# Loading every fifth x tile in three pieces of 100, 20 and 8 rows on fewer DMA engines

## The chip, the cores and the metric

The kernel runs on one core of one Trainium2 chip. A core has a matmul engine (PE), a vector engine (DVE), a scalar engine (ACT), a queue engine (SP) and sixteen DMA engines that carry every transfer between device memory (DRAM) and on-chip memory (SBUF). The metric is device time in microseconds, as a median of several runs. Every run below was fast, that is, within 1.5% of the fastest run of the same kernel. A profiled span is 1.2 to 2.4 us shorter than the timed median of the same kernel, so I compare spans with spans and times with times.

## The reference, cut to what matters

```python
i_idx, j_idx = np.triu_indices(32, k=1)          # 496 pairs of 32 fields
vi = inputs[:, i_idx, :]                         # inputs: (4096, 32, 64)
vj = inputs[:, j_idx, :]
vdotw = jnp.einsum('bpd,pde->bpe', vi, W)        # W: (496, 64, 64)
return (vdotw * vj).reshape(B, -1)               # (4096, 31744), float32
```

The output is 520 MB. The inputs are 33.6 MB (x) and 8.1 MB (W). Each pair needs one small matrix product and one elementwise product.

## The kernel before

The batch is cut into 32 tiles of 128 rows. For each tile, x is loaded to SBUF, transposed by PE, and multiplied with the weights. DVE multiplies the product in PSUM (PE's output memory) by x and writes it to a ring (a buffer that is filled in turn and used again) in SBUF, and five stores take the tile from the ring to DRAM. ACT issues the x loads; SP issues the weight loads and the stores. The ring holds a little under one tile's output (28160 of 31744 columns), so DVE has to wait until an old store has landed before it may write over its place. There are two x buffers.

```python
STORES = [[0, 1], [2, 3], [4, 5], [6, 7, 8], [9, 10, 11, 12, 13, 14, 15]]
PREFETCH_AT = [5, 6]
RING = 28160
...
    def load_x(t):
        xt = xpool.tile([P, F * D], F32, tag="x", name=f"x_{t}")
        nc.scalar.dma_start(out=xt, in_=x[ts(t, P), :])
        return xt
...
    xs = {0: load_x(0)}
    for p in range(NPR):
        ...                                             # 16 weight loads on SP
    for t in range(NT):
        xt, xT = xs.pop(t), xTs.pop(t)
        if t + 1 < NT:
            xs[t + 1] = load_x(t + 1)
        for s, group in enumerate(STORES):
            ...
            for p in group:
                if t + 1 < NT and p in PREFETCH_AT:
                    transpose_x(...)                    # the next tile's x, on PE
                ...                                     # matmuls, DVE products into the ring
            nc.sync.dma_start(out=out[ts(t, P), o0 : o0 + store_w[s]], in_=osb)
```

Of the kernel before, what the change touches and what calls it, by code (L numbers as in the profile page):

```python
# [1 line left out]

# [6 lines left out]

F32 = mybir.dt.float32  # L10
ALU = mybir.AluOpType

P = 128
BANK = 512

STORES = [[0, 1], [2, 3], [4, 5], [6, 7, 8], [9, 10, 11, 12, 13, 14, 15]]
PREFETCH_AT = [5, 6]
RING = 28160


@with_exitstack
def pair_bilinear_kernel(
    ctx: ExitStack,
    tc: tile.TileContext,
    x: bass.AP,
    w: bass.AP,
    out: bass.AP,
    F: int,
    D: int,
):  # L30
















    nc = tc.nc
    B = x.shape[0]
    NT = B // P
    NPR = F // 2  # L50

    width = [(F - 1 - i) * D for i in range(F)]
    off = [sum(width[:i]) for i in range(F)]
    woff = [sum(width[0 : 2 * p : 2]) for p in range(NPR)]
    store_w = [sum(width[2 * p] + width[2 * p + 1] for p in g) for g in STORES]

    const = ctx.enter_context(tc.tile_pool(name="const", bufs=1))
    xpool = ctx.enter_context(tc.tile_pool(name="x", bufs=2))
    xtpool = ctx.enter_context(tc.tile_pool(name="xT", bufs=2))
    psum = ctx.enter_context(tc.tile_pool(name="ps", bufs=4, space=bass.MemoryType.PSUM))  # L60

    ident = const.tile([P, P], F32, tag="ident", name="ident")
    make_identity(nc, ident)

    def runs(tl, a, b, n):

        ap = tl[:, a : a + n]
        return bass.AP(ap.tensor, ap.offset, [list(ap.ap[0]), [b - a, 2], list(ap.ap[1])])

    def load_x(t):  # L70
        xt = xpool.tile([P, F * D], F32, tag="x", name=f"x_{t}")
        nc.scalar.dma_start(out=xt, in_=x[ts(t, P), :])
        return xt

    def transpose_x(xT, t, xt, g):

        n = 2 * BANK // P
        pt = psum.tile([P, 2 * BANK], F32, tag="ps", name=f"pt_{t}_{g}")
        for c in range(n):
            nc.tensor.transpose(pt[:, ts(c, P)], xt[:, ts(n * g + c, P)], ident)  # L80
        nc.scalar.copy(xT[:, ts(g, 2 * BANK)], pt)  # L81

    def new_xT(t):
        return xtpool.tile([P, NPR * P], F32, tag="xT", name=f"xT_{t}")

    ring = const.tile([P, RING], F32, tag="ring", name="ring")
    at = 0
    xs = {0: load_x(0)}

    w_sb = []  # L90
    for p in range(NPR):
        wp = const.tile([P, width[2 * p]], F32, tag=f"w{p}", name=f"w{p}")
        nc.sync.dma_start(out=wp, in_=w[:, woff[p] : woff[p] + width[2 * p]])
        w_sb.append(wp)

    xTs = {0: new_xT(0)}
    for g in range(2):
        transpose_x(xTs[0], 0, xs[0], g)
# [6 lines that stand above are left out]
            if at + store_w[s] > RING:  # L105
                at = 0
            osb = ring[:, at : at + store_w[s]]
            at += store_w[s]
            o0 = off[2 * group[0]]
            for p in group:  # L110
                if t + 1 < NT and p in PREFETCH_AT:
                    if t + 1 not in xTs:
                        xTs[t + 1] = new_xT(t + 1)
                    transpose_x(xTs[t + 1], t + 1, xs[t + 1], PREFETCH_AT.index(p))
                for c0 in range(0, width[2 * p], BANK):
                    pm = psum.tile([P, 2, BANK], F32, tag="ps", name=f"pm_{t}_{p}_{c0}")
                    n = [max(0, min(BANK, width[2 * p + h] - c0)) for h in range(2)]
                    for h in range(2):
                        if n[h]:
                            nc.tensor.matmul(  # L120
                                pm[:, h, : n[h]],
                                xT[h * D : (h + 1) * D, ts(p, P)],
                                w_sb[p][h * D : (h + 1) * D, c0 : c0 + n[h]],
                                start=True,
                                stop=True,
                            )
                    o = [off[2 * p + h] - o0 + c0 for h in range(2)]
                    xj = [(2 * p + h + 1) * D + c0 for h in range(2)]
                    if n[0] == n[1]:
                        nc.vector.tensor_tensor(  # L130
                            runs(osb, o[0], o[1], n[0]),
                            pm[:, :, : n[0]],
                            runs(xt, xj[0], xj[1], n[0]),
                            ALU.mult,
                        )
                    else:
                        for h in range(2):
                            if n[h]:
                                nc.vector.tensor_tensor(  # L139
                                    osb[:, o[h] : o[h] + n[h]],  # L140
                                    pm[:, h, : n[h]],
                                    xt[:, xj[h] : xj[h] + n[h]],
                                    ALU.mult,
                                )
            nc.sync.dma_start(out=out[ts(t, P), o0 : o0 + store_w[s]], in_=osb)


# [33 lines left out]
```

## Time and profile before

| | before |
|---|---|
| time, median | 1341.3 us |
| span of the profiled run | 1339.7 us |
| DMA, mean share of sixteen engines | 98.8% |
| DVE, PE busy | 88%, 86% |
| last engine's end after the others' | 10.3 to 10.7 us |

The DMA share is a mean over sixteen engines and cannot tell whether one of them is behind. For that, each engine has to be read by itself; the prediction below tells how the packet records are laid end to end into sixteen chains. In each chain the stores come in program order, eight rows and a small semaphore packet (it reports the landing) for each store, and this settles most ambiguities. Where two chains are at the same point at the same nanosecond they may be swapped; the slow one can be told by its long rows. A chain has no number: numbers of engines in this document come from the skill's rule for which engines a load uses, which the prediction cites, and no trace shows them.

### The profile page before, as it was taken

Reading aid. Unit: us, or ns where it says so; the run is one execution under the profiler, and the core shown is the slowest. Engines: PE = TensorE matmul, PEld = TensorE weight load, DVE = VectorE, ACT = ScalarE, POOL = GpSimd, SP = SyncE. Lnnn points to the kernel's source line nnn. Section 1 sums busy time; section 2 is a strip of 40 time slices with the busy share of each in tenths; the row PEclk is TensorE's granted clock in tenths of the full one; section 3 lists DMA queues with packets and bytes.
Section 4 is the critical chain, followed back from the end, with each engine's and each line's share of the span. In section 5 each row is a group of like instructions: output and inputs, shape, how many; then the busy total and the mean of one; then the engine's idle time right before and its main releaser. Section 6 shows DMA issues by size and latency. Waiting matters only on the chain.

```text
span 1339.7 us, 13755 instructions
## 1 busy us (share of the span) xinstructions
PE 1151.0 (86%) x5376; PEld 548.7 (41%) x5376; DVE 1177.4 (88%) x1664; ACT 66.1 (5%) x65; POOL 0.7 (0%) x6
## 2 busy tenths in 40 slices
PE   7998889888898888988888978889798897888992
PEld 3444344443343443443433534444344443444441
DVE  6999889888899988989888989899898997898993
ACT  1000000000000000000000000000000000000000
POOL 0000000000000000000000000000000000000000
PEclk9999889999999999989999899899898998998996
DMA  9999999999999999999999999999999999999996
GB/s 392 426 431 434 429 431 429 427 427 434 426 434 430 422 422 430 422 424 429 415 426 424 426 426 404 415 420 431 428 420 408 431 427 431 416 424 420 422 429 264
DMA packets 30017, 562.93 MB, mean 420 GB/s; under 512 B 3456, under 2 KB 3840, under 8 KB 5376
## 3 DMA queue, kind: packets, MB, share of 16 engines
q1 hardware_dynamic: 25344, 528.49, 92.6%
q10 hardware_dynamic: 4608, 33.56, 6.0%
q8 instruction: 42, 0.69, 0.2%
q14 instruction: 23, 0.19, 0.0%
HBM read 41.94 MB, written 520.09 MB: 420 GB/s over the span
## 4 chain that ended last, share of the span: by engine, by line
DMA 54%; DVE 23%; PE 11%; issue 9%; DVEq 0%
DMA out_dram<-ring 54%; DVE ring L130 15%; PE pm L120 9%; DVE ring L139 9%; PE pt L80 2%; DMA x<-in_x_dram 1%; DVEq L130 0%; DVEq L177 0%
## 5 line engine op out<-in xcount | busy, mean ns | idle before, releaser
L120 PE MATMUL pm<-w,xT 64*128 64x512 f32 (+7 forms) x4864 | 1083.2, 559 | 158.3 <-DVE ring L130 140.1
L130 DVE TENSOR_TENSOR ring<-pm,x 128x1024 f32<-128x1024 f32 x768 | 904.0, 1217 | 138.4 <-DMA out_dram<-ring 93.0
L120 PEld LDWEIGHTS pm<-w,xT 64*128 64x128 f32 x4864 | 487.7, 194 | 720.1 <-DVE ring L130 451.3
L139 DVE TENSOR_TENSOR ring<-pm,x 128x448 f32<-128x448 f32 (+6 forms) x896 | 330.2, 415 | 3.6 <-PE pm L120 2.9
L81 ACT COPY xT<-pt 128x1024 f32<-128x1024 f32 x64 | 64.8, 1012 | 1194.6 <-PE pt L80 1194.6
L80 PE MATMUL pt<-ident,x 128*128 128x128 f32 x512 | 76.5, 297 | 8.5 <-DMA x<-in_x_dram 8.5
L80 PEld LDWEIGHTS pt<-ident,x 128*128 128x128 f32 x512 | 61.0, 152 | 48.9 <-issue 35.3
L81 ACT ACT_TABLE_LOAD x1 | 1.3, 1283 | 1.7 <-PEq L173 1.7
masks.py:199 POOL TENSOR_SCALAR_AFFINE_SELECT ident<-ident 128x128 f32<-128x128 f32 x1 | 0.3, 292 | 0.1
masks.py:197 POOL MEMSET ident<- 128x128 f32 x1 | 0.2, 204 | 0.3 <-POOLq L173 0.3
L173 POOL MEMSET const-bfloat16-1.0<- 128x1 bf16 x1 | 0.1, 101 | 0.0
L173 POOL MEMSET const-uint8-127<- 128x1 uint8 x1 | 0.1, 101 | 0.0
L173 POOL MEMSET const-float32-0.0<- 128x1 f32 x1 | 0.1, 98 | 0.2 <-issue 0.2
L173 POOL MEMSET const-float32-1.0<- 128x1 f32 x1 | 0.1, 98 | 0.0
## 6 DMA issues: line engine op xcount, KB each, us to landing
out_dram<-ring SPq DMA_DIRECT2D x32, 3776.0 KB, 22.8
out_dram<-ring SPq DMA_DIRECT2D x32, 3264.0 KB, 21.8
out_dram<-ring SPq DMA_DIRECT2D x32, 3168.0 KB, 22.4
out_dram<-ring SPq DMA_DIRECT2D x32, 2912.0 KB, 22.3
out_dram<-ring SPq DMA_DIRECT2D x32, 2752.0 KB, 22.1
x<-in_x_dram ACTq DMA_DIRECT2D x32, 1024.0 KB, 14.2
w<-in_w_dram SPq DMA_DIRECT2D x1, 992.0 KB, 7.4
w<-in_w_dram SPq DMA_DIRECT2D x1, 928.0 KB, 11.7
```

Of the source, the lines that this page charges most:

```text
L80: nc.tensor.transpose(pt[:, ts(c, P)], xt[:, ts(n * g + c, P)], ident)
L81: nc.scalar.copy(xT[:, ts(g, 2 * BANK)], pt)
L120: nc.tensor.matmul(pm[:, h, : n[h]], xT[h * D : (h + 1) * D, ts(p, P)], w_sb[p][h * D : (h + 1) * D, c0 : c0 + n[h]], start=True, stop=True,)
L130: nc.vector.tensor_tensor(runs(osb, o[0], o[1], n[0]), pm[:, :, : n[0]], runs(xt, xj[0], xj[1], n[0]), ALU.mult,)
L139: nc.vector.tensor_tensor(osb[:, o[h] : o[h] + n[h]], pm[:, h, : n[h]], xt[:, xj[h] : xj[h] + n[h]], ALU.mult,)
L173: nc = bacc.Bacc("TRN2", target_bir_lowering=False, num_devices=1)
```

## The change

The intent to be read from it is to take load from the highest six DMA engines, in seven of the 32 tiles (1, 6, 11, 16, 21, 26, 31), and to give it to the lowest ten. The bytes stay the same.

```diff
+FEW = 5
+FEW_ROWS = [100, 20, 8]
...
-        nc.scalar.dma_start(out=xt, in_=x[ts(t, P), :])
+        r0 = 0
+        for n in FEW_ROWS if t % FEW == 1 else [P]:
+            nc.scalar.dma_start(out=xt[r0 : r0 + n, :], in_=x[t * P + r0 : t * P + r0 + n, :])
+            r0 += n
```

## The prediction

> **What bounds the kernel now.** I read the page's slices, queue rows and chain first, to see which resource is full; then the waits of the vector engine and of the store queue, to see who waits for whom; then the stretches; and last the packet records themselves, engine by engine.
>
> ```profile
> span 1339.7 us, 13755 instructions
> DMA  9999999999999999999999999999999999999996
> q1 hardware_dynamic: 25344, 528.49, 92.6%
> q10 hardware_dynamic: 4608, 33.56, 6.0%
> HBM read 41.94 MB, written 520.09 MB: 420 GB/s over the span
> DMA 54%; DVE 23%; PE 11%; issue 9%; DVEq 0%
> DMA out_dram<-ring 54%; DVE ring L130 15%; PE pm L120 9%; DVE ring L139 9%; PE pt L80 2%; DMA x<-in_x_dram 1%; DVEq L130 0%; DVEq L177 0%
> x<-in_x_dram ACTq DMA_DIRECT2D x32, 1024.0 KB, 14.2
> ```
>
> The DMA engines are busy in every slice but the last. q1 (stores and w) takes 92.6% of the time of sixteen engines, q10 (x) 6.0%; with 0.2% of instruction fetch that is 98.8%, or 1323.6 us of 1339.7 on the mean engine. The chain names a store in 54% of the span. PE (86%) and DVE (88%) come after it.
>
> ```profile
> DVE ring L130 <- DMA out_dram<-ring: 93.0, 53, 3.3
> DVE ring L130 <- PE pm L120: 45.4, 52, 13.2
> ...
> SPq L145 <- DVE ring L139: 1228.7, 159, 10.5
> ```
>
> The vector engine waits for ring space (a store's landing) 53 times, 93.0 us in all. The store queue then waits for the vector engine. So a store that lands late holds back the next store: the last of its sixteen shares counts.
>
> ```profile
> core 0: us, PE busy (x) PEld busy (x) DVE busy (x) ACT busy (x) POOL busy (x), PEclk, DMA share, GB/s
> 9.00:50.00 41.00, 38.49 (x189) 19.58 (x189) 36.55 (x53) 4.05 (x4) 0.00 (x0) 1.00 1.02 423
> 50.00:500.00 450.00, 395.49 (x1852) 189.03 (x1850) 405.39 (x574) 22.27 (x22) 0.00 (x0) 0.95 1.00 429
> 500.00:1000.00 500.00, 438.90 (x2048) 208.53 (x2045) 448.21 (x632) 24.29 (x24) 0.00 (x0) 0.95 0.99 422
> 1000.00:1320.00 320.00, 277.63 (x1292) 130.97 (x1292) 287.22 (x409) 14.17 (x14) 0.00 (x0) 0.95 0.99 422
> 1320.00:1340.00 20.00, 0.00 (x0) 0.00 (x0) 0.00 (x0) 0.00 (x0) 0.00 (x0) 0.56 0.39 169
> ```
>
> In these rows by stretch the DMA share is 1.00 and 429 GB/s up to 500 us, 0.99 and 422 GB/s from there. In the last 20 us no compute engine works and the DMA share is 0.39, so most engines are done while something still drains.
>
> The packet records do not name their engine, but one engine's packets follow each other within 4 ns, so I laid all 30030 end to end into sixteen chains (a reconstruction; fast chains may be swapped among themselves, a slow one is told by its durations). **One chain is slow and fifteen are alike.** The slow one is busy 1344.2 us, never idle once data flows, and ends last. The other fifteen are busy 1318.7 to 1325.1 us (mean 1321.9), idle 10.6 us on the mean in 9 to 23 pauses, the first at about 495 us of the span, and all end 10.3 to 10.7 us before the slow one. A store row of 30208 B takes 1155 ns on the slow engine and 1119 to 1125 on the others (3% more), one of 22016 B 843 against 820; an x row of 8192 B 314 against 309. The slow engine loses some 0.75 us per batch tile, the ring hides a skew of about 10 us, and after tile 12 the others wait for it. The 22.3 us between 1344.2 and 1321.9 are about the 10.6 us of pauses and the 10.5 us of tail.
>
> **What the Trainium skill says.** (1) "DMA: Bandwidth & Descriptors", section "Why a DMA increments its semaphore by 16 and not by 1": a DMA issued by SP or ACT runs on the largest k up to 16 that divides the slowest dimension, and on the lowest-numbered k; its example is 100 partitions on 10 engines. So 100, 20 and 8 rows run on engines 0-9, 0-9 and 0-7. The trace before has only 128-row loads, on sixteen. (2) Same page, "Latency and other measured facts": engines 7 and 15 are usually slower, with a best guess that ties it to software descriptor rings. The trace agrees that an engine is slow, but only one, and there is no software queue in it; which number it has the trace doesn't say. (3) Same page, "Where 436 GB/s comes from": 435.2 GB/s over sixteen ports, so 27.2 each. The fast engines' 30208 B in 1119 ns are 27.0: each engine is at its own ceiling, so rows cannot be sped up, only moved. (4) "SBUF — State Buffer", section "Door 1: The DMA port swizzle": the partitions decide which of sixteen ports a transfer uses. In the pieces several engines may write to one port; no run yet shows what it costs.
>
> **The change part by part.** No byte and no compute instruction is added. Tiles 1, 6, 11, 16, 21, 26 and 31, seven of 32, have three x loads in place of one. The instruction order shows 14 more on ACT, and none else.
> - Removed: the six highest engines lose 8 rows in each of seven tiles: 56 x 0.309 = 17.3 us (56 x 0.314 = 17.6 us on the slow engine).
> - Added: engines 0-7 get 10 + 2 + 1 = 13 rows for 8, so 7 x 5 x 0.309 = 10.8 us; engines 8 and 9 get 12, so 7 x 4 x 0.309 = 8.7 us.
> - Issues: 14 x 0.37 us on ACT, which is busy 5%: nothing. The semaphores of the pieces were used last by transfers of the tile before last, 41 us earlier, against a landing time of 22 us: no wait. At the start the third piece of tile 1 goes out after the copies at 13 us and is wanted at 30 us.
> - Moved: x comes later. Eight rows between store rows take 8.5 to 9.2 us, about 1.08 each, after some 5 us; thirteen make 5 + 14 = 19 us.
>
> ```profile
> 620.63 0.36 ACTq L72 DMA_DIRECT2D x<-in_x_dram  x1
> 644.21 1.01 ACT L81 COPY xT<-pt 128x1024 f32<-128x1024 f32 x1 [38.85 <-PE pt L80]
> ...
> 705.07 0.37 ACTq L72 DMA_DIRECT2D x<-in_x_dram  x1
> 723.83 1.01 ACT L81 COPY xT<-pt 128x1024 f32<-128x1024 f32 x1 [33.22 <-PE pt L80]
> ```
>
> In this timeline the copy follows eight transposes (1.1 us), so x is wanted 22.5 us after its issue in one tile and 17.6 in another. PE may wait up to 2 us in some of the seven tiles. DVE has 1340 - 1177 = 163 us to spare, 5 per tile, and two stores are in flight, so this should not reach the DMA engines.
>
> The sum rests on a choice: I take the slow engine to be among the six highest (the page says 7 or 15, and the change would be odd otherwise). Then its work falls to 1344.2 - 17.6 = 1326.6 us, and it would end 17.6 us earlier. Engines 0-7 rise to 1321.9 + 10.8 = 1332.7 us on the mean and become the bound: 1344.2 - 1332.7 = 11.5 us earlier than the slow one ended. The same by the ends: 10.5 us of tail, plus 10.6 us of pauses that go since the skew stays under what the ring hides, less 10.8 us, is 10.3 us. The busiest fast chain (1325.1, with fetches on it) would leave 8 us. Two things pull further, which I set against each other: rows of 23296 B took 865 ns on the fast engines in the first nine tiles and some 895 later, when the pauses had begun, so up to 4 us may come back; and the moved rows may take longer, or x may come late. I take 8.5 us, near the busiest chain: 1341.3 - 8.5 = 1332.8, so **1333 us**.
>
> **The rivals.**
> - *The slow engine is one of the lowest ten*, 7 for instance. It is then given 35 x 0.314 = 11 us more: 1352 us. For it: the skill names 7 as well. Against: one slow chain only, and the period of five fits a gap of 22 us for a high engine (it closes 17.6 + 10.8 = 28). Chance 1 in 7.
> - *The moved rows collide*: ten engines write partitions that several share by port, and the 7 x 128 = 896 moved rows (896 x 0.309 / 10 = 28 us on each of ten) take, say, a fifth longer, 5.5 us; or late x starves the stores. Then most of the gain is gone: 1338 to 1343 us. For it: the rows have no such layout before. Against: an x row is less than a third of an engine's time while x loads.
> - *Perfect balance*: all engines end at the mean, 1323.3 us of busy time for 1344.2 on the slow one, 21 us less: 1320 us at the very best. Nothing can give more, as each row is at its engine's ceiling.
>
> **Range and chances.** Over 2% faster means under 1314.5 us, below the mean busy time: all but excluded. Over 2% slower means 1368 us: it needs a low slow engine and collisions on top, 2%. The middle is 1333; 1327 is the 10 to 11.5 us of the sum with the 4 us of late rows on top; 1343 is the gain lost to collisions. The rival at 1352 (1 in 7) lies outside, which is most of the fifth that I leave out.
>
> **What would show it.** Right: the six high engines have x rows in 25 of 32 tiles, the slow chain is one of them, with busy time near 1327; the pauses and the 10 us tail of draining shrink; the share stays 1.00 after 500 us; DVE's 93.0 us of waiting for stores falls a little. Wrong if the slow chain carries 13-row loads, if x rows in the pieces take clearly over 309 ns, or if PE waits for x by tens of us.

## More of the kernel before

Tile 0 and tile 1 of x load at the start, beside the weights. From tile 2 on an x load has only stores beside it.

The records name the chip of each experiment: e1 to e4 ran on chip 3, e5 to e7 on chip 10, e8 and e9 on chip 5; for the first pair none is named. Each round had the kernel before beside it, and it took 1341.2 to 1341.35 us on all of them.

## The result, and the profile after

The changed kernel takes **1357.45 us** (1357.31 to 1357.88, four runs) against 1341.32 us in the same rounds: 16.1 us slower. The ratio is 1.012, with a 95% interval of 1.0103 to 1.0138. Ratios here are the mean time of one kernel's fast runs over that of the other's of the same rounds, so not quite the ratio of the medians that I quote. The class "within 2%" was right; the time lies outside the predicted range, and the sign was wrong.

From the page of the changed kernel (the span, the queue rows, the chain by line, and the x loads by size):

```profile
span 1355.2 us, 13789 instructions
...
q1 hardware_dynamic: 25344, 528.49, 92.2%
q10 hardware_dynamic: 4692, 33.56, 6.1%
...
HBM read 41.94 MB, written 520.09 MB: 415 GB/s over the span
...
DMA out_dram<-ring 51%; DVE ring L137 13%; PE pm L127 9%; DVE ring L146 8%; DMA x<-in_x_dram 5%; PE pt L87 2%; ACTq L78 0%; DVEq L137 0%; DVEq L184 0%
...
x<-in_x_dram ACTq DMA_DIRECT2D x25, 1024.0 KB, 14.2
x<-in_x_dram ACTq DMA_DIRECT2D x7, 800.0 KB
x<-in_x_dram ACTq DMA_DIRECT2D x7, 160.0 KB
```

The shares of the queues are as high as before in a span that is 15.5 us longer. The engines are still full, and yet they move only 415 GB/s for 420. The bytes are equal; q10 has 84 more packets, all of them the small semaphore packets of the pieces.

The first 33.5 us of the kernel before, by the view of stretches (its first slice in the page):

```profile
0.00:33.50 33.50, 24.16 (x111) 12.19 (x111) 20.34 (x25) 4.32 (x4) 0.70 (x6) 1.00 0.98 392
```

The same stretch of the changed kernel:

```profile
0.00:33.50 33.50, 22.28 (x100) 13.10 (x102) 18.56 (x22) 3.60 (x4) 0.70 (x6) 0.95 0.96 318
```

The last two numbers are the DMA share and the GB/s. The engines are as busy, at 318 instead of 392 GB/s, and DVE gets 22 products done instead of 25. In the run e2 below, which has the change in tile 1 alone, the clock of PE (the third number from the end) is 1.00 as before and the stretch is as slow, so the 0.95 of the changed kernel is not the cause:

```profile
0.00:33.50 33.50, 22.65 (x104) 12.66 (x106) 19.29 (x24) 4.32 (x4) 0.70 (x6) 1.00 0.95 318
```

The waits of the SP queue for the landing of weights say the same as the GB/s. First before, then after (time in total, times, longest):

```profile
SPq L93 <- DMA w<-in_w_dram: 11.7, 7, 3.8
```

```profile
SPq L100 <- DMA w<-in_w_dram: 21.6, 8, 6.5
```

The packet records show what is slow in that stretch. The 128 x rows of tile 1 take 466 ns on the mean instead of 309, and the weight rows take 58 us longer in total (74.9 us over their shortest durations instead of 16.6). With the 20 us of the x rows that is 78 us over sixteen engines, or 4.9 us on each.

After the start the rest of the loss builds up on one chain. This is the slow chain from its first store row on, by the packet records:

```
          first store row   end       from one to the other   idle        x rows in tiles 6,11,16,21,26,31
before    27.8              1338.4    1310.6                  under 1     8 each
after     34.3              1353.8    1319.5                  under 1     13 each
(us from the start of the span; the other fifteen idle 10.7 us on the mean before, 14.4 after, and end
10.3 to 10.7 us before the slow one before, 10.2 to 10.4 after, one of them 8.5)
```

The slow chain starts its stores 6.5 us later and then needs 8.9 us more: 15.4 us, all but 0.1 of the difference of the spans. **The slow chain carries 13 x rows in every one of the six later tiles of the change, and in tile 1 too.** So the slow engine is one of those that were given more; by the skill's rule these 13 rows are on engines 0 to 7.

The vector engine's waits after:

```profile
DVE ring L137 <- DMA out_dram<-ring: 85.1, 53, 4.4
DVE ring L137 <- PE pm L127: 68.5, 61, 13.6
```

Its wait for stores fell from 93.0 to 85.1 us, which alone would look like a gain. Its wait for PE rose from 45.4 to 68.5 us, and PE's own wait for x from 8.5 to 20.6 us:

```profile
PE pt L87 <- DMA x<-in_x_dram: 20.6, 4, 8.7
```

Such sums of waits do not rank two kernels; the end of the slowest chain does.

### The profile page after: what moved, and what is told of

The parts are those of the page before. It is cut to its first block, busy times and chain, and to the rows that moved or that the text cites. A ratio compares the mean times of both kernels' runs of the same rounds, so it can differ in the third digit from the quotient of the medians.

```text
span 1355.2 us, 13789 instructions
## 1 busy us (share of the span) xinstructions
PE 1155.9 (85%) x5376; PEld 552.9 (41%) x5376; DVE 1178.1 (87%) x1664; ACT 66.1 (5%) x65; POOL 0.7 (0%) x6
## 4 chain that ended last, share of the span: by engine, by line
DMA 56%; DVE 22%; PE 11%; issue 9%; ACTq 0%; DVEq 0%
DMA out_dram<-ring 51%; DVE ring L137 13%; PE pm L127 9%; DVE ring L146 8%; DMA x<-in_x_dram 5%; PE pt L87 2%; ACTq L78 0%; DVEq L137 0%; DVEq L184 0%
## 5 line engine op out<-in xcount | busy, mean ns | idle before, releaser
L137 DVE TENSOR_TENSOR ring<-pm,x 128x1024 f32<-128x1024 f32 x768 | 906.0, 1220 | 153.6 <-DMA out_dram<-ring 85.1
L87 PE MATMUL pt<-ident,x 128*128 128x128 f32 x512 | 79.1, 305 | 22.6 <-DMA x<-in_x_dram 20.6
## 6 DMA issues: line engine op xcount, KB each, us to landing
out_dram<-ring SPq DMA_DIRECT2D x32, 2912.0 KB, 23.1
```

What stands on the lines that cost most here:

```text
L87: nc.tensor.transpose(pt[:, ts(c, P)], xt[:, ts(n * g + c, P)], ident)
L137: nc.vector.tensor_tensor(runs(osb, o[0], o[1], n[0]), pm[:, :, : n[0]], runs(xt, xj[0], xj[1], n[0]), ALU.mult,)
```

## The experiments

Theory A says that two things cost the 16 us. The slow engine is among the lowest eight, and each row more on it adds 0.314 us; and in tile 1, which loads beside the weights, the pieces make engines collide. The rivals are an equal cost of the layout in all seven tiles (B), the start alone (C), and, for the start, more DMAs sharing the same few semaphores (S). The diffs are against the changed kernel, with unchanged lines left out.

**e1_not_first: tile 1 as before.**

```diff
-        for n in FEW_ROWS if t % FEW == 1 else [P]:
+        for n in FEW_ROWS if t % FEW == 1 and t > 1 else [P]:
```

> The change in six tiles only; tile 1, which loads while the weights load, keeps one load on sixteen engines. Theory A (the slow engine is one of the lowest eight, and the start collides): the first store rows are back at their time of before, six tiles give the slow engine 6 x 5 x 0.314 = 9.4 us: 1341.3 + 9.4 = 1350.7 us. Rival B (all 16 us come in equal parts from the seven tiles, by their layout or by late x): 6/7 of 16 us, 1355 us. Rival C (all comes from the start): 1341 us.

Measured: 1350.75 us against 1341.35; ratio 1.007 (1.0055 to 1.0085). The loss of 9.4 us is what A gave; B (1355) and C (1341) fall. The start is back: the stretch from 9 to 50 us moves 423 GB/s, and the first store rows of the chains begin at 27.5 to 28.2 us of the span (27.7 to 28.2 before). The slow chain has 13 x rows in each of the six tiles, is idle for less than 1 us, and needs 8.6 us more than before from its first store row to its end.

**e2_first_only: the change in tile 1 alone.**

```diff
-        for n in FEW_ROWS if t % FEW == 1 else [P]:
+        for n in FEW_ROWS if t == 1 else [P]:
```

> The change in tile 1 only. Theory A: 1.6 us for five more rows on the slow engine and some 4.7 us for the collisions at the start: 1341.3 + 6.3 = 1347.6 us. Rival B (equal parts): 1343.6 us. Rival C (all from the start): 1357 us.

Measured: 1347.69 us; ratio 1.0048 (1.0033 to 1.0063). The loss is 6.3 us, as in A. The two parts add up: 9.4 + 6.3 = 15.7 of 16.1 us. So two fifths of the loss come from one tile out of seven.

**e3_columns: three pieces of columns, each of 128 rows on sixteen engines.**

```diff
-        r0 = 0
-        for n in FEW_ROWS if t % FEW == 1 else [P]:
-            nc.scalar.dma_start(out=xt[r0 : r0 + n, :], in_=x[t * P + r0 : t * P + r0 + n, :])
-            r0 += n
+        c0 = 0
+        for n in [1024, 512, 512] if t % FEW == 1 else [F * D]:
+            nc.scalar.dma_start(out=xt[:, c0 : c0 + n], in_=x[ts(t, P), c0 : c0 + n])
+            c0 += n
```

> All seven tiles load x in three pieces, but of columns (1024, 512, 512), each of 128 rows on sixteen engines, so as many DMAs and semaphores as in the change, without its imbalance and with the partitions of before for each engine. If the start is late because more DMAs share the semaphores (rival S), some 4.7 us stay: 1346 us, and the first store row stays 5 us late. If it is late because engines write into each other's partitions (theory A), nothing stays: 1341 to 1342 us, with the x rows of tile 1 at their shortest duration.

Measured: 1342.8 us; ratio 1.001 (0.9994 to 1.0027), the same as before within the interval. The number of DMAs and of semaphores is that of the change, and the start is whole. From 9 to 50 us, in the view of stretches of this run:

```profile
9.00:50.00 41.00, 38.49 (x189) 19.56 (x188) 36.31 (x51) 4.05 (x4) 0.00 (x0) 1.00 1.03 424
```

So S falls as the cause of the late start. The remaining 1.5 us are not explained; PE waits for x 64.4 us in this run, which the pieces of columns bring late in some tiles.

**e4_rows16: three pieces of rows, but with all sixteen engines at 8 rows.**

```diff
-FEW_ROWS = [100, 20, 8]
+FEW_ROWS = [64, 48, 16]
```

> All seven tiles in three pieces of 64, 48 and 16 rows, each on sixteen engines, so 8 rows on every engine as before, but with other partitions for each engine than in the loads of 128 rows. Theory A: no imbalance is left, the collisions at the start stay: 1341.3 + 3 to 6, 1344 to 1347 us, with x rows of tile 1 clearly over 309 ns. If the imbalance made the start late too: 1341.3 us.

Measured: 1349.25 us; ratio 1.006 (1.0045 to 1.0075). No engine has more rows than another, and the start is slow again:

```profile
9.00:50.00 41.00, 38.58 (x186) 19.20 (x184) 35.36 (x48) 4.05 (x4) 0.00 (x0) 1.00 1.02 376
```

The x rows of tile 1 take 549 ns, and the first store rows begin at 32.6 us instead of 27.7. The clock is 1.00 here too. Together with e3 this shows that pieces of rows make the start slow, without any imbalance, and that the number of DMAs does not. The loss is 7.9 us, over the 3 to 6 that I expected: in tiles 21, 26 and 31 x rows also took 419 to 440 ns. By its packet records the slow chain starts 5.1 us late and needs 3.1 us more after that. Why the last tiles suffer most, and tiles 6 (310 ns), 11 (355 ns) and 16 (341 ns) less, is open.

**e5_seven_few: is it engine 7, one of the two numbers that the skill names?**

```diff
-FEW_ROWS = [100, 20, 8]
+FEW_ROWS = [119, 7, 2]
...
-        for n in FEW_ROWS if t % FEW == 1 else [P]:
+        for n in FEW_ROWS if t in (6, 14, 22, 30) else [P]:
```

> Four tiles (6, 14, 22, 30) load x in pieces of 119, 7 and 2 rows, on the seven, seven and two lowest engines: 18 rows on engines 0 to 6 (19 on 0 and 1), none on 7 to 15. The packet records of the changed kernel put the slow chain among the eight lowest engines; this tells 7 from 0-6. If it is engine 7: it loses 4 x 8 x 0.314 = 10 us, engines 0 and 1 gain 4 x 11 x 0.309 = 13.6 us, within the 21 us that they wait or end early now, so 1341.3 - 7.5 to 10 = 1331 to 1334 us, some us more if x comes too late in these tiles. If it is one of 0 to 6: 4 x 10 x 0.314 = 12.6 us more, 1354 us.

Measured: 1353.53 us; ratio 1.0091 (1.0076 to 1.0107). It fits "one of 0 to 6", but the run was badly designed and I do not rest on its time. Eighteen rows for an engine bring x too late, PE waits for it, and most DMA engines run dry: in the page's GB/s row, four slices, those of the four tiles, fall to 347 to 353.

```profile
PE pt L87 <- DMA x<-in_x_dram: 51.6, 5, 11.8
```

The packet records of the run say more than its time: the slow chain carries 18 x rows in each of the four tiles and is itself idle for less than 1 us. By the rule only engines 2 to 6 have 18.

**e6_seven_often and e7_eight_often: the same question with one row at a time.** Both move rows in the fifteen even tiles from 2 on. The diff is that of e6; e7 has [112, 8, 8] in its place.

```diff
-FEW_ROWS = [100, 20, 8]
+FEW_ROWS = [112, 7, 7, 2]
...
-        for n in FEW_ROWS if t % FEW == 1 else [P]:
+        for n in FEW_ROWS if t % 2 == 0 and t > 1 else [P]:
```

> The fifteen even tiles from 2 on load x in pieces of 112, 7, 7 and 2 rows, on sixteen, seven, seven and two engines: 7 rows on engines 7 to 15, 9 on 2 to 6, 10 on 0 and 1. If the slow engine is number 7: 15 x 0.314 = 4.7 us less, 1336.6 us. If it is one of 0 to 6: 4.7 us more (9.4 for 0 or 1), 1346 us or over. Collisions of the moved rows in the later tiles may add 1 to 3 us to either, as in the run with 64, 48 and 16 rows.

> The control of the run before it: the same fifteen tiles in pieces of 112, 8 and 8 rows, on sixteen, eight and eight engines: 9 rows on engines 0 to 7, 7 on 8 to 15. If the slow engine is any of 0 to 7: 15 x 0.314 = 4.7 us more, 1346 us, also where the run with seven gets faster. If it is none of them: 4.7 us less, 1336.6 us. The same 1 to 3 us of collisions may come on top.

Measured: 1346.94 us (ratio 1.0043, 1.0028 to 1.0057) and 1347.17 us (ratio 1.0045, 1.0028 to 1.0061). They are alike, 5.7 and 6.0 us slower than the kernel before at 1341.2. In both the slow engine has one row more per tile (4.7 us), and about 1 us comes on top. So engine 7 is not it on this chip: it was relieved in e6 and the time went up. The packet records agree: the slow chain carries 9 x rows in each of the fifteen tiles of both runs, and in e6 only engines 2 to 6 have 9.

**e8_staircase: which of 0 to 6.**

```diff
-FEW_ROWS = [100, 20, 8]
+FEW_ROWS = [112, 6, 5, 4, 1]
...
-        for n in FEW_ROWS if t % FEW == 1 else [P]:
+        for n in FEW_ROWS if t % 2 == 0 and t > 1 else [P]:
```

> Which of engines 0 to 6 is slow. Fifteen even tiles in pieces of 112, 6, 5, 4 and 1 rows. Against 8 rows before, engine 0 has 11, engines 1 to 3 have 10, engine 4 has 9, engine 5 has 8, engines 6 to 15 have 7. With 15 x 0.314 us for each row, and about 1 us of collisions as in the two runs with 7 and 8 rows: slow engine 0, 1356 us; 1, 2 or 3, 1352 us; 4, 1347 us; 5, 1342 us; 6, 1338 us.

Measured: 1347.41 us; ratio 1.0046 (1.0029 to 1.0063), where 1347 stood for engine 4. The packet records say it without a time: the slow chain carries 9 x rows in 14 of the 15 tiles (in the last the laying of the chains is not certain to one row). By the rule only engine 4 has 9 rows in this kernel. **The slow engine is number 4**, shown for chip 5 and by way of that rule. On chip 10 the record leaves engines 2 to 6 (e5 and e6), and on chip 3 engines 0 to 7 (13 rows in e1). That it is the same engine on all of them is likely and not shown.

**e9_four_often: the row taken from engine 4.**

```diff
-FEW_ROWS = [100, 20, 8]
+FEW_ROWS = [112, 4, 4, 4, 4]
...
-        for n in FEW_ROWS if t % FEW == 1 else [P]:
+        for n in FEW_ROWS if t % 2 == 0 and t > 1 else [P]:
```

> The same tiles in pieces of 112, 4, 4, 4 and 4 rows: 11 rows on engines 0 to 3, 7 on all others. Slow engine among 0 to 3: 45 x 0.314 = 14 us more and 1 of collisions, 1356 us. Slow engine 4, 5 or 6: 4.7 us less and 1 of collisions, 1337 to 1338 us, as engines 0 to 3 have 21 us to give and get 14: this would be faster than both kernels.

Measured: **1338.12 us** (1337.66 to 1339.35) against 1341.22; ratio 0.9978 (0.9963 to 0.9992). This is faster than both kernels, by 0.2% against the one before, and it is the kind of sum that I had made for the change, done on the right engines: the slow chain carries 7 rows in each of the fifteen tiles (one row in one tile is not certain) and ends at 1334.3 us of the span instead of 1338.4. The next chain now ends 1.2 us before it instead of 10.3, so there is little left to give to the four engines that took the rows. DVE's wait for stores, in this run:

```profile
DVE ring L137 <- DMA out_dram<-ring: 39.4, 24, 3.0
```

It fell from 93.0 us to 39.4. PE's wait for x rose to 54.5 us, and this did not cost the gain.

## Why the prediction was wrong

- **What bounds the kernel** was right. One chain of packets has store rows 3% slower than the rest, is idle for less than 1 us, and ends 10 us after them; in all experiments the time moved as the end of this chain moved.
- **The failed step** is the sentence "I take the slow engine to be among the six highest". It rested on two things that were no measurements: the skill's "7 or 15", and the thought that "the change would be odd otherwise", backed by a period that seemed to fit a gap of 22 us. The slow chain carried the 13-row loads, so it got 7 x 5 rows more instead of losing 7 x 8; by e8 it is number 4. The skill's two numbers already put one of two on the low side, so 1 in 7 was low on its own ground. The prediction had no view in which the engine's number could be seen, said so, and went on as if it had one.
- **Removed and added rows**: the arithmetic held with the sign turned. Six tiles of five rows at 0.314 us are 9.4 us, and e1 measured 9.4. Its profiled span is 8.7 us longer, so that both agree to a tenth is luck.
- **The rival "the slow engine is one of the lowest ten"**, at 1352 us and a chance of 1 in 7, was right in its mechanism. Its sum left out the start, which cost about 4.9 us more: 1341.3 + 11 + 4.9 = 1357.2, with 1357.45 measured; this sum was made after the result.
- **The rival "the moved rows collide"** was right for one tile and mis-sized. I spread a fifth of a row's time over all tiles. In tile 1 the rows took 466 ns for 309, and slowed the weights with them; in tiles 6, 11 and 16 they took 310 to 314 ns; in tiles 21, 26 and 31 they took 355 to 372. That the cause is engines writing to one port, as the rival says, was not shown. The step that failed is the one at the start: "the third piece of tile 1 goes out after the copies at 13 us and is wanted at 30 us" looked only at when x is wanted, not at what it does to the weight loads beside it.
- **Rows at their ceiling**: the 27.2 GB/s is worked out for a port, and that it holds for an engine is an inference. The traces fit it: 1119 ns is the shortest time of a 30208 B row in ten of the eleven traces, and 1116 ns in e1.
- **Issues and semaphores cost nothing**: right for the start, by e3; over the whole run at most e3's 1.5 us. The issues themselves were not the 0.37 us of the sum: on ACT the longest took 1.64 us.
- **Late x** was right in kind. PE waited for x four times, 20.6 us in all; before it was once, 8.5 us at the start. In e1 it waited 23.1 us, and the loss there is that of the rows, so these waits cost nothing that could be seen.
- **What would show it**: I had written that 13-row loads on the slow chain would prove me wrong, and they did. The share after 500 us stayed at 0.99 and did not rise to 1.00, since the other engines went on waiting for the slow one.

## What to carry to other kernels

This kernel, which keeps its DMA engines full, ran at the pace of the slowest one, and a mean share of 98.8% hid that. In such a kernel, find which engine it is by giving the engines unequal rows and counting the rows on the slow chain, before moving any load. Pieces of rows that cost little beside stores (about 1 us for fifteen tiles in e6 and e7, 3.1 us for six in e4) cost about 5 us in the one tile that loads beside the weights, so ask for each transfer what else is in flight. A number from a page, or a guess at what a change was made for, is a place to look; until a run has shown it, the range of a forecast should hold both cases.

## What the Trainium skill lacked or had wrong

- "DMA: Bandwidth & Descriptors", section "Latency and other measured facts", names engines 7 and 15 as usually slower. In this kernel one engine is slower, and it is neither of these: e6, on chip 10, relieved both and became slower, and e8, on chip 5, gives number 4 by the page's own rule. In the kernel before it took 1156 ns for a stored row of 30208 B, against 1119 to 1125 on the fifteen others. There is no software queue in the program, which the page has as its best guess of a cause. Why this engine is slow no run here shows.
- The same page, section "Why a DMA increments its semaphore by 16 and not by 1", gives the rule for k and the lowest-numbered engines. The runs agree as far as they go: all rows on the slow chain fit one engine, number 4, with 13 for pieces of 100, 20 and 8, 18 for 119, 7 and 2, 9 for 112, 6, 5, 4 and 1, and 7 for 112, 4, 4, 4 and 4. No trace shows the numbers themselves. The page does not say that a chain's rows can be used to find an engine's number.
- "SBUF — State Buffer", section "Door 1: The DMA port swizzle", explains the ports but gives no size for collisions between loads with different splits. Here loads of rows in pieces beside the weight loads took 466 ns a row (549 in e4) for 309, and the core moved 318 GB/s for 392 in the first 33.5 us. That the ports are the reason fits e3 and e4, but was not shown.
